# Loading x with four neighbouring tokens per partition, and putting the transposed tile back into token order as it leaves PSUM

## The chip, the cores and the metric

The kernel runs on one core of a Trainium2 chip. The metric is the device time of one execution in microseconds (us). A core has a matrix engine (PE; its weight loads are listed apart as PEld), a vector engine (DVE), a scalar engine (ACT), a general engine (POOL) and a sequencer that issues DMAs (SP). ACT and POOL can issue DMAs too. Data lies in HBM, is worked on in SBUF (128 partitions), and matrix products arrive in PSUM, which is used here as eight banks of 128 x 512 floats. Everything is float32.

## What is computed

x has 32 batches of 512 tokens with 256 channels, adj is a 512 x 512 matrix of zeros and ones per batch. With one layer norm in front, a graph layer is added to x:

```python
h = jnp.maximum(_layernorm(x, axis=-1), 0.0)
x = x + _L0_gnn_ref(h, adj, ...)
# inside the layer, with h as x:
xc = transpose(x, (0, 2, 1))
c = relu(bn1(conv1d(xc, conv1_w, 0)))            # 1 tap: a product per token
c = bn2(conv1d(c, conv2_w, 8))                   # 17 taps along the tokens
x_conv = transpose(relu(c + xc), (0, 2, 1))
s = x @ w_se.T + b_se                            # 3 numbers per token
A = exp(-|s_n - s_m|^2) * mask
x_nmp = A @ relu(x @ w_msg.T + b_msg)
# then a GRU cell: gates from x_in = [x_conv, x_nmp] and from x, out = (1 - z) * n + z * x
```

Two things of this matter for the change. The layer norm works on each token alone, so it doesn't matter in which partition a token lies. The 17-tap convolution runs along the tokens, so what comes after the transposition needs the tokens in their order.

## The kernel before

The batches are worked in two groups of 16 (g = 0 and 1, `GB` = 16). Each group has a first part (`first_part`, L1167) and a node part (`nodes`, L1322). After both groups a last part makes the gates and the output for pairs of batches. Tiles and names: P = 128, NC = 4 chunks of 128 tokens, DC = 2 halves of 128 channels, N = 512 tokens, D = 256 channels.

The first part does, for each batch:

- `load_x` (L213): one DMA of 512 KB brings x of the batch into a tile of 128 partitions x 4 chunks x 256 channels. Token c * 128 + p lies in partition p, chunk c. So a partition receives four runs of 1 KB. The loads of batches 1 to 5 and of 16 to 18 are issued by SP, the other 23 by POOL. Batch 0 is loaded in three pieces (L1298, L1299): chunk 0 and chunks 2 to 3 by SP, chunk 1 by ACT.
- `statistics` (L388): DVE takes mean and variance of each token (L392 four times, L394 four times, L397), and POOL raises the variance to the power -1/2 (`rstd`, L398).
- `normalise` (L400): xn = (x - mean) * rstd, four instructions on DVE (L411). In batches 0 (two chunks) and 17 (all four), ACT does it (L409).
- `transpose_h` (L414): PE transposes xn by 128 x 128 blocks, eight in all (L419, tile phT), four into each of two PSUM banks. So a bank holds 128 channels x 512 tokens, chunk after chunk. DVE moves each bank to SBUF and takes the maximum with 0 (L423, tile hT). For the second half of batch 0 ACT does it (L421). SP then stores hT to HBM (L424, tile hd), from where later parts read it.
- `conv1` (L430): 16 matrix products with hT as stationary side (L439, tile pc), moved out by DVE with an addition (L442, tile h), then made positive by ACT (L443).
- `windows_to_freq` (L447): 16 products that take the tokens into another domain for the 17-tap convolution (L454, tile px), moved out by ACT (L457, tile xf).

In group 0 the steps of `weights_to_freq` (L353) stand between these: they bring the convolution's weights into the same domain (PE L363, tile pw; moved out by ACT L373 and DVE L371, tile wst; stored by SP L377). In group 1 four leftover products of the first group (py, L503) and sums of weights on POOL and ACT (L1272) stand there.

The order is written out by hand (`manual_schedule`, L1316 and L1453); nothing is reordered. In a round b of group 1 the calls are: statistics of batch b + 2, transposition of batch b + 1, normalisation of b + 2, `conv1` of b, `windows_to_freq` of b - 1. On DVE that makes: stats (b + 2), hT (b + 1), xn (b + 2), h (b). On PE: phT (b + 1), pc (b), px (b - 1). Each engine takes its instructions in order, and waits for another engine by semaphores. `load_x` of batch b + 3 is issued at the head of round b. PSUM's eight banks are handed out in turn; such a round takes eight (two phT, two pc, four px).

Later parts load x of a batch again, in a layout of their own (tile xb); those loads are not those of `load_x`.

Of the kernel before, what the change touches and what calls it, by code (L numbers as in the profile page):

```python
# [12 lines left out]
AF = mybir.ActivationFunctionType  # L13
ALU = mybir.AluOpType

P = 128
# [146 lines left out]
def gnn_layer(  # L163
# [15 lines left out]
    nc = tc.nc  # L179
# [5 lines left out]
    NC = N // P  # L185
# [16 lines left out]
    def bank(name):  # L202
        return psum.tile([P, N], FP, tag="bank", name=name)

    X, ADJ, XN, HT, HQ, H1, MSG, A, NMP, ST, SL, SR = ({} for _ in range(12))
# [6 lines left out]

    def load_x(b, queue=nc.sync):  # L213
        X[b] = pools["ahead" if b == GB else "first"].tile([P, NC, D], FP, tag="x", name=f"x_{b}", bufs=1 if b == GB else 3)
        queue.dma_start(X[b], x[b].rearrange("(c p) d -> p c d", p=P))


    ident = consts.tile([P, P], FP, name="ident")
# [66 lines left out]
    def load_w1():  # L285

        t = W2P["w1"] = pools["gen"].tile([P, PI, D], FP, tag="w2p", name="w1_in", bufs=2)
        load_rows(t[:, :DC], w1T, nc.sync)
# [57 lines left out]
    def load_taps(gen, pc, queue=nc.gpsimd):  # L346
        t = W2P[pc] = gen.tile([P, PI, D], FP, tag="w2p", name=f"w2p_{pc}", bufs=2)
        src = w2T.rearrange("(q i) k o -> q k i o", q=4)[:, :, PI * pc : PI * (pc + 1)]
        for q in range(4):
            queue.dma_start(t[32 * q : 32 * q + 16], src[q, 0:16])  # L350
        queue.dma_start(t[16::32], src[:, 16])
# [62 lines left out]
    def transpose_h(b):  # L414
        HT[b] = work.tile([P, DC, N], FP, tag="hT", name=f"hT_{b}")
        for dc in range(DC):
            p = bank(f"phT_{b}_{dc}")
            for c in range(NC):
                nc.tensor.transpose(p[:, c * P : (c + 1) * P], XN[b][:, c, dc * P : (dc + 1) * P], ident)  # L419
            if b == 0 and dc > 0:  # L420
                nc.scalar.activation(HT[b][:, dc, :], p, AF.Relu)  # L421
            else:
                nc.vector.tensor_scalar(HT[b][:, dc, :], p, 0.0, None, op0=ALU.max)  # L423
        nc.sync.dma_start(HD[b], HT[b])  # L424
        del XN[b]

# [740 lines left out]
    def first_part(g, freq, between, left=()):  # L1167
# [3 lines left out]
        for b in range(b0, b0 + 3):  # L1171
            if b not in X and (g == 0 or b == b0):
                load_x(b)
# [22 lines left out]
        if g > 0:  # L1196
            place_h1(b0)
            load_x(b0 + 1)
            fill()
            load_x(b0 + 2)  # L1200
        transpose_h(b0)
        statistics(b0 + 1)
        fill()
# [4 lines left out]
        for b in range(b0, b1):  # L1208
            if b + 3 < b1:
                load_x(b + 3, nc.sync if b < 3 else nc.gpsimd)  # L1210
            if b == b0:
                conv1(b)
                one, two = between(0) if g == 0 else ([], [])
                for step in one:
                    step()
                fill()
                if g == 0:
                    transpose_h(b + 1)
                    statistics(b + 2)
                    normalise(b + 2)  # L1220
                else:
                    normalise(b + 2)
                    transpose_h(b + 1)
                fill()
                xf, last_two = freq(g), two
                continue
# [54 lines left out]
    @contextmanager  # L1281
    def phase(*names, bufs=1):
        with ExitStack() as stack:
            for name in names:
                pools[name] = stack.enter_context(tc.tile_pool(name=name, bufs=bufs, reuse_waits="tile"))
            yield

    with tc.tile_pool(name="freq", bufs=1) as fpool:
# [3 lines left out]
        with phase("first", "gen"):  # L1292
            gen = pools["gen"]
            per = N // D
            steps = [partial(weights_to_freq, gen, pc, i) for pc in range(QI // PI) for i in range(0, PI, per)]

            X[0] = pools["first"].tile([P, NC, D], FP, tag="x", name="x_0", bufs=3)
            for queue, c0, c1 in ((nc.sync, 0, 1), (nc.scalar, 1, 2), (nc.sync, 2, NC)):  # L1298
                queue.dma_start(X[0][:, c0:c1, :], x[0, c0 * P : c1 * P, :].rearrange("(c p) d -> p c d", p=P))  # L1299
            load_w1()  # L1300
            load_x(1)
            load_taps(gen, 0, nc.sync)
            nc.sync.dma_start(taps, nc.inline_tensor(taps_np, name="dft_taps").ap())
            nc.sync.dma_start(fwd, nc.inline_tensor(fwd_np, name="dft_fwd").ap())

            def between(b):
                if 1 <= b <= len(load_weights):
                    load_weights[b - 1]()

                n = (2, 0, *(3 if b in (12, 14) else 2 for b in range(2, GB)))[b]  # L1310
                mine = [[steps.pop(0)] for _ in range(n)]
                if b % 2 == 0 and b // 2 + 1 < QI // PI:
                    mine[b > 0].insert(0, partial(load_taps, gen, b // 2 + 1))
                return (mine[0], mine[1:]) if b == 0 else mine

            with tc.manual_schedule():  # L1316
                xf = first_part(0, freq_tile, between)
# [232 lines left out]
```

## Time and profile before

| | |
|---|---|
| time, median of three runs | 1731.43 us (1731.42 to 1732.1) |
| the profiled execution's own time | 1730.94 us |
| its span, first to last instruction | 1729.2 us |
| L423, hT from PSUM, DVE, 128 x 512 | 63 instructions, mean 685 ns |
| L421, hT from PSUM, ACT, 128 x 512 | 1 instruction, 597 ns |
| L411, xn, DVE, 128 x 256 | 122 instructions, mean 452 ns |
| L392, stats, DVE, 128 x 256 | 128 instructions, mean 410 ns |
| L442, h from PSUM, DVE, 128 x 512 | 64 instructions, mean 683 ns |
| x, issue of a load on POOL (L215) | 23, median 798 ns |
| x, issue of a load on SP (L215) | 8, median 431 ns |
| x, from issue to landing | median 6.4 us (3.7 to 9.5) |
| idle time of DVE that ended with a landing of x | 10.5 us, 10 times |

The page of the profile gives the busy time of each engine, the span in 40 slices, the DMA queues, the chain of work that ended last, and the costliest groups of instructions with their mean duration and with the idle time just before them. Further views of the same execution list instructions in order of time, the waits by what ended them, and the busy time of the engines in chosen stretches. A busy PE is not a PE at its peak, as matrix products overlap. An instruction's duration includes its start-up, and the next one of the same engine can begin before it ends: two of the 685 ns take 1.29 us together. The first part of group 0 takes about 0 to 150 us, that of group 1 about 424 to 535 us.

### The profile page before, as it was taken

What the parts mean: (1) busy time and instruction counts of PE and PEld (TensorE: products, weight loads), DVE (VectorE), ACT (ScalarE), POOL (GpSimd) and SP (SyncE); (2) the same over time, 40 slices, a digit from 0 to 9 for tenths busy, and PEclk for the clock granted to TensorE, in tenths of its full rate; (3) what the DMA queues carried; (4) which work ended last, traced back from release to release, by engine and by line L of the source; (5) the groups of instructions that cost most, each with busy time, mean ns of one, the idle gap of its engine ahead of it and who ended that gap; (6) DMA issues with size and microseconds to landing.
All of it is one profiled execution on the core that took longest, in us unless ns stands there. A gap on an engine that the chain in (4) does not pass through costs nothing.

```text
span 1729.2 us, 24317 instructions
## 1 busy us (share of the span) xinstructions
PE 1715.6 (99%) x7920; PEld 1321.8 (76%) x7920; DVE 1304.2 (75%) x2599; ACT 692.2 (40%) x1669; POOL 1087.2 (63%) x1074
## 2 busy tenths in 40 slices
PE   9999999999999999999999999999999999999998
PEld 6777888888998888887877778777877787778754
DVE  7876877777996677666587778777887778777867
ACT  4556655553446555554323232232313331323221
POOL 3331787687655677777767657665667556755551
PEclk9999999999999999999999999999999999999999
DMA  9989987885878888898433454335523553345423
GB/s 256 301 279 264 262 232 240 259 228 181 275 245 230 268 241 246 230 257 305 120 103 74 80 128 113 73 72 128 128 66 67 125 128 87 75 96 128 111 55 73
DMA packets 311681, 295.07 MB, mean 171 GB/s; under 512 B 147436, under 2 KB 241164, under 8 KB 311172
## 3 DMA queue, kind: packets, MB, share of 16 engines
q1 hardware_dynamic: 301588, 265.17, 55.9%
q0 software_dynamic: 6960, 26.65, 4.9%
q10 hardware_dynamic: 3008, 1.72, 0.3%
q8 instruction: 63, 1.03, 0.3%
q14 instruction: 62, 0.51, 0.1%
HBM read 194.31 MB, written 99.16 MB: 170 GB/s over the span
## 4 chain that ended last, share of the span: by engine, by line
PE 95%; DVE 3%; DMA 1%; SPq 1%; POOL 1%; ACT 0%; issue 0%; DVEq 0%; POOLq 0%; ACTq 0%
PE pg L915 29%; PE pn L932 16%; PE py L503 11%; PE pn L670 10%; PE pm L558 6%; PE pc L439 6%; PE pc L878 4%; PE px L454 3%; PE pd L608 2%; PE pw L363 1%; PE phT L419 1%; PE pg L932 1%; PE pz L932 1%; PE pc L881 1%; PE pn L653 1%; DVE xn L411 0%
## 5 line engine op out<-in xcount | busy, mean ns | idle before, releaser
L470 POOL TENSOR_TENSOR wsum<-wt 128x512 f32<-128x512 f32 x66 | 94.2, 1427 | 99.6 <-DMA wt<-wd 64.0
L503 PE MATMUL py<-wt,xf 128*128 128x256 f32 x640 | 154.2, 384 | 0.0
L915 PE MATMUL pg<-te,sw 128*128 128x256 f32 x600 | 154.0, 379 | 0.0
L906 ACT ACTIVATE rz<-rz,brz 128x256 f32<-128x256 f32 x180 | 86.4, 504 | 146.7 <-DVE rz L921 146.7
L503 PEld LDWEIGHTS py<-wt,xf 128*128 128x128 f32 x640 | 117.1, 190 | 34.9 <-issue 19.7
L915 PEld LDWEIGHTS pg<-te,sw 128*128 128x128 f32 x600 | 114.0, 190 | 15.5
L915 PE MATMUL pg<-hn,sw 128*128 128x256 f32 x480 | 123.2, 379 | 0.0
L915 PE MATMUL pg<-tn,sw 128*128 128x256 f32 x480 | 123.2, 379 | 0.0
L618 DVE TENSOR_TENSOR A<-A,at 128x512 f32<-128x512 f32 x124 | 116.6, 979 | 6.4 <-ACT A L614 2.8
L932 PE MATMUL pn<-tn,sw_n 128*128 128x512 f32 x256 | 120.3, 592 | 0.0
L1077 ACT ACTIVATE pn<-nt,vech 128x512 f32<-128x512 f32 x45 | 31.1, 692 | 219.2 <-DVE nt L1074 139.8
L439 PE MATMUL pc<-w,hT 128*128 128x256 f32 x512 | 117.5, 382 | 0.9 <-DVE hT L423 0.9
L558 PE MATMUL pm<-wmsg,hq 128*128 128x259 f32 x512 | 117.4, 381 | 0.0
L439 PEld LDWEIGHTS pc<-w,hT 128*128 128x128 f32 x512 | 94.7, 190 | 23.6 <-issue 6.4
L812 POOL TENSOR_TENSOR tn<-hn 128x512 f32<-128x512 f32 x64 | 87.1, 1382 | 35.5 <-PE pn L932 35.5
L558 PEld LDWEIGHTS pm<-wmsg,hq 128*128 128x128 f32 x512 | 96.5, 189 | 14.6
L915 PEld LDWEIGHTS pg<-hn,sw 128*128 128x128 f32 x480 | 91.1, 190 | 18.3 <-PE pn L932 3.3
L915 PEld LDWEIGHTS pg<-tn,sw 128*128 128x128 f32 x480 | 91.2, 190 | 12.4
L921 DVE TENSOR_TENSOR ct<-pg,ct 128x256 f32<-128x256 f32 x180 | 74.8, 415 | 32.5 <-PE pg L915 22.7
L932 PEld LDWEIGHTS pn<-tn,sw_n 128*128 128x128 f32 x256 | 48.6, 190 | 61.2 <-issue 50.9
L932 PE MATMUL pn<-hn,sw_n 128*128 128x512 f32 x192 | 90.5, 593 | 0.2 <-DVE pn L1073 0.2
L915 PE MATMUL pg<-tec,sw 128*128 128x256 f32 x300 | 89.2, 379 | 0.0
(235 smaller groups left out, 4331.4 us busy)
## 6 DMA issues: line engine op xcount, KB each, us to landing
wt<-wd SPq DMA_DIRECT2D x80, 512.0 KB, 6.2
adj<-in_adj_dram SPq DMA_DIRECT2D x128, 256.0 KB, 5.8
wd<-wst SPq DMA_DIRECT2D x64, 320.0 KB, 5.5
yd<-y SPq DMA_DIRECT2D x76, 256.0 KB, 5.1
hd<-hT SPq DMA_DIRECT2D x32, 512.0 KB, 4.9
nd<-nmp SPq DMA_DIRECT2D x32, 512.0 KB, 3.0
xb<-in_x_dram SPq DMA_DIRECT2D x128, 128.0 KB, 6.1
out_dram<-xb SPq DMA_DIRECT2D x122, 128.0 KB, 2.8
```

The source lines that it names most:

```text
L439: nc.tensor.matmul(p[:, j, :], HT[b][:, ic, c * P : (c + 1) * P], w1[:, ic, :], start=(ic == 0), stop=(ic == DC - 1))
L470: nc.gpsimd.tensor_tensor(t, WT[g, u][:, 0], WT[g, u][:, 1], op=ALU.add)
L503: nc.tensor.matmul(dst, v[:, ic, :], w[:, ic, :], start=(ic == 0), stop=(ic == DC - 1))
L558: nc.tensor.matmul(p[:, : D + NS], hq[:, ic, c * P : (c + 1) * P], wmsg[:, ic, :], start=(ic == 0), stop=(ic == DC - 1))
L618: nc.vector.tensor_mul(A[b][:, mc, :], EXP.pop((b, mc)), AT.pop((b, mc)))
L670: nc.tensor.matmul(bk, left[:, k, :], right[:, k, :], start=(first and k == 0), stop=(k == 1), skip_group_check=True)
L812: nc.gpsimd.tensor_tensor(dst[:, k], x[:, k], y[:, k], op=op)
L878: nc.tensor.matmul(bk[:, t0:t1], YT[p][:, j, c, oc * P : (oc + 1) * P], back[:, n : n + t1 - t0], start=(c == 0), stop=False, skip_group_c ...
L906: nc.scalar.activation(at(dst), at(src), AF.Sigmoid, bias=brz[:, o : o + 1], scale=sign)
L915: nc.tensor.matmul(bk, SW["hk"][:, k, s, :], c if k == 2 else hn[:, k], start=(onto is None and k == 0), stop=(k == K3 - 1), skip_group_ch ...
L921: nc.vector.tensor_tensor(at(dst), at(x), at(y), op=op)
L932: nc.tensor.matmul(bk[:, t], weight(q, k, o), terms[k][q][:, t], start=(first and i == 0), stop=(i == len(ks) - 1), skip_group_check=True)
```

## The change

In the SBUF tile of x, partition p now holds the four neighbouring tokens 4p to 4p + 3: token 4p + c lies in chunk c. In HBM these are 4 KB in one run. Layer norm and transposition are done as before on this tile, so a PSUM bank of phT now holds the tokens in the order 0, 4, 8, ..., 508, 1, 5, ... The instruction that moves it to SBUF reads PSUM straight through and writes column m of chunk c to token 4m + c: neighbouring elements of its stream are written four floats apart. hT is as it was before, and so is everything after it. The three pieces of batch 0's load keep their chunks, and take them from the same rearranged view.

```diff
     def load_x(b, queue=nc.sync):
...
-        queue.dma_start(X[b], x[b].rearrange("(c p) d -> p c d", p=P))
+        queue.dma_start(X[b], x[b].rearrange("(p c) d -> p c d", p=P))
...
                 nc.tensor.transpose(p[:, c * P : (c + 1) * P], XN[b][:, c, dc * P : (dc + 1) * P], ident)
+            dst, src = HT[b][:, dc, :].rearrange("p (m c) -> p c m", c=NC), p.rearrange("p (c m) -> p c m", c=NC)
             if b == 0 and dc > 0:
-                nc.scalar.activation(HT[b][:, dc, :], p, AF.Relu)
+                nc.scalar.activation(dst, src, AF.Relu)
             else:
-                nc.vector.tensor_scalar(HT[b][:, dc, :], p, 0.0, None, op0=ALU.max)
+                nc.vector.tensor_scalar(dst, src, 0.0, None, op0=ALU.max)
...
             for queue, c0, c1 in ((nc.sync, 0, 1), (nc.scalar, 1, 2), (nc.sync, 2, NC)):
-                queue.dma_start(X[0][:, c0:c1, :], x[0, c0 * P : c1 * P, :].rearrange("(c p) d -> p c d", p=P))
+                queue.dma_start(X[0][:, c0:c1, :], x[0].rearrange("(p c) d -> p c d", p=P)[:, c0:c1, :])
```

The order of the instructions on each engine, their number and what they wait for are the same in both programs.

## The prediction

> **What bounds the kernel now.** I read the page's first parts first. The profiled execution took 1730.94 us, of which 1729.2 us are the span; 1.7 us lie around it. The median of the three runs shown is 1731.43, 0.5 us (0.03%) above it. My sum is made against 1730.94.
>
> ```profile
> span 1729.2 us, 24317 instructions
> PE 1715.6 (99%) x7920; PEld 1321.8 (76%) x7920; DVE 1304.2 (75%) x2599; ACT 692.2 (40%) x1669; POOL 1087.2 (63%) x1074
> ```
>
> PE has 13.6 us of idle in all, so there is little to gain anywhere. What can be lost must be read per stage: the changed lines run only in the two first parts, 0 to 150 us (batches 0 to 15) and 424 to 530 us (16 to 31). So I asked for the busy time of each engine in stretches there (columns: stretch, its length, then PE, PEld, DVE, ACT, POOL busy, clock, DMA share, GB/s).
>
> ```profile
> 20.00:40.00 20.00, 19.41 (x118) 13.95 (x115) 19.84 (x58) 10.44 (x24) 7.37 (x10) 1.00 0.95 268
> 453.40:516.70 63.30, 63.30 (x389) 59.17 (x388) 60.69 (x171) 29.78 (x85) 41.30 (x73) 1.00 0.76 266
> ```
>
> DVE, 75% over the span, is 99% busy in the first and 96% in the second of these stretches (and 93% to 99% in the 20 us slices from 440 to 520). There it is a second bound beside PE. The chain of work that ended last, cut to the first 60 us, shows DVE as the bound before 34.5 us (start, length, what):
>
> ```profile
> 15.33 1.19 DVE hT L423 x2
> 16.52 1.31 DVE stats L392 x4
> ...
> 23.88 1.29 DVE hT L423 x2
> ...
> 29.41 1.29 DVE hT L423 x2
> ...
> 33.93 0.48 ACT wst L373
> 34.41 0.04 issue
> 34.46 1.14 PE phT L419 x8
> ```
>
> Up to 34.46 the chain steps from DVE to DVE, and the evictions hT (L423) of batches 1, 2 and 3 are links of it. From there to 150 us it is mostly PE, whose pieces of one batch (phT 0.87, pc 3.65, px 2.37, two pw 1.03) sum to 8.95 us, against 7.2 us of DVE work (busy 54.57 us from 72 to 140, which is 7.6 batches). In the second first part the chain is all PE, one batch in 6.50 us:
>
> ```profile
> 459.65 0.87 PE phT L419 x8
> 460.53 3.46 PE pc L439 x16
> 463.98 2.17 PE px L454 x16
> 466.16 0.87 PE phT L419 x8
> ```
>
> From the start of batch 21's statistics (453.35) to that of batch 31's (516.68), by the timeline, DVE does ten batches with 60.69 us busy: 6.07 us each against PE's 6.50. That margin of 0.43 us per batch is the number on which all turns. The timeline shows how tight the coupling is: batch 21's xn (L411) ends at 459.16 and PE's transposes, which need it, start at 459.36.
>
> ```profile
> 457.15 2.01 DVE L411 TENSOR_SCALAR xn<-x,mv,rstd 128x256 f32<-128x256 f32 x4 [0.62 <-POOL rstd L398]
> 459.36 0.93 PEld L419 LDWEIGHTS phT<-ident,xn 128*128 128x128 f32 x8
> ```
>
> **The change, part by part.** No instruction is added, removed or moved on any engine; only the access patterns differ.
>
> *Loads of x.* Thirty-one loads of 512 KB become one 4 KB run per partition in place of four of 1 KB. Most wait nowhere: DVE idles for x 10.5 us in all (10 times), and PE waits for none of it except in the first 9 us. The loads from POOL, 23 of these 31, already travel as large packets:
>
> ```profile
> q0 software_dynamic: 6960, 26.65, 4.9%
> ```
>
> 26.65 MB in 6960 packets is 3.8 KB each; 23 loads at 1 KB would be 11776 packets alone. In the trace's packets 1 KB takes 46 ns and 4 KB 159 ns (medians), so a load from SP goes from 32 x 46 = 1.47 to 8 x 159 = 1.27 us per DMA engine: 0.2 us, beside PE. An issue on POOL (0.80 us) may come near that of other large POOL loads (hn 0.72 to 0.74): 0.06 us ahead of the rstd queued behind it. The first tile's three pieces keep 1 KB (two) and get 2 KB (one; 84 ns against 2 x 46); its statistics start at 2.98 and 4.41 us and PE waits for them, so here -0.2 to +0.3 us. The rest of the gain is bounded by PE's lost time that is near x: four batches from 34.46 to 71.77 take 37.3 us against 4 x 8.95 = 35.8, so 1.5 us at the most. I take 0 for the loads, with ends -1.7 and +0.3.
>
> *Evictions of the transposed tile.* 63 on DVE (L423, mean 685 ns) and one on ACT (L421, 597 ns) now write each 4-byte element 16 bytes from the last. Reads from PSUM stay contiguous. The trace has no such write of any length. Its rows:
> - DVE fills: contiguous 128 elements 165 ns, 16 elements each 32 bytes apart 72 ns.
>
> ```profile
> L326 DVE MEMSET fl<- 128x128 f32 x1 | 0.2, 165 | 0.8 <-PEq L1538 0.8
> L328 DVE MEMSET fl<- 128x16 f32 x1 | 0.1, 72 | 0.0
> ```
>
> A DVE element costs 1.05 ns by the 512- and 256-wide PSUM evictions (L442 683, L561 414 ns: 269 over 256). Sixteen contiguous ones would then take 165 - 112 x 1.05 = 47 ns; the strided fill took 25 more, 1.5 ns an element. For 512 elements that is +0.79 us per eviction: the upper end. Small instructions also carry some 40 ns that lines through large ones miss (L397, 4 elements, 169 ns at least, against 395 - 252 x 1.05 = 130 from L411's shortest), so the fill does not exclude +0.
> - ACT's xf copy (L457) reads PSUM 320 bytes apart and writes runs of four: 438 ns for 320 elements, on the line through its 256- and 512-wide copies (L677 374 and L655 587 give 427). [...]
>
> I take c = +0.54 us per eviction (512 x 1.05, a second step for each element), the round value between these ends that is nearest to the only DVE row with a strided write; ends 0 and 0.79.
>
> [...]
>
> **The sum for c = 0.54.** *First part:* batch 0's DVE eviction ends 0.21 us before the next statistics, which waited for x: 0.54 - 0.21 = 0.33. Then the six evictions of batches 1 to 3 stand in the chain: 6 x 0.54 = 3.24. Batch 0's ACT eviction runs beside DVE: its users (pc of batch 0, then h at 14.05) come behind xn of batch 1, so 0. From batch 4 on, two evictions make the 7.2 us of DVE per batch 8.3, against 8.95: covered by PE. With 0.65 us less of that cover they would begin to be paid. Sum 3.6.
>
> *Second part:* the eviction of batch 20 lies ahead of xn of batch 21. Its 1.08 is met by the 0.62 us in which xn waited for POOL's rstd, and by 0.2 to 0.33 before PE's transposes: 0.13 is left. Then each of ten batches needs 6.07 + 1.08 = 7.15 us of DVE, 71.5 in all, where PE took 65.0 from phT of batch 21 to phT of 31: 6.5. Batches 17 to 19 have gaps (DVE waited 1.62, 1.13 and 0.64 us for x between 426 and 454) that take their part, and hT of batch 31 ends at 526.44, with pc at 531.0: covered. Sum 6.6.
>
> Behind a slower eviction on SP stand the store hd (L424) and, behind that, stores of wst and early x loads; the store waits for DVE, and x of batch 3 and 4 is used by the same delayed DVE, so they add nothing. PSUM: the bank of a phT is asked for by PE a batch later, for transposes that need an xn which stands behind this eviction on DVE anyway: 0.
>
> Total 3.6 + 6.6 = +10.2 us: 1730.94 + 10.2 = **1741.1**.
>
> **Rivals.**
> 1. *The strided write runs at full rate (c under about 0.3), so not slower.* At c = 0 DVE is as before; loads give -1.7 to +0.3: 1729.2 to 1731.2. Decides: the total passes 3.5 us (0.2%) near c = 0.3 (first part 7 x 0.3 - 0.21 = 1.9, second 10 x (6.07 + 0.6) - 65.0 = 1.7). For it: ACT's xf row, small-instruction overhead in the fill.
> 2. *The fill's full price, c = 0.79.* First part 0.58 + 4.74 = 5.3; second 10 x (6.07 + 1.58) - 65.0 + (1.58 - 0.95) = 12.1: 1748.3.
> 3. *The loads do more than I allow (faster).* Every wait for x that reaches PE would have to vanish, and some that the profile doesn't show, as 1.7 is under 3.5. Against it: PE 99%, packets on q0 already large.
> That the change doesn't do what it says is part of rival 1: for POOL's loads the larger runs may change nothing, being packets of that size now.
>
> **How the numbers follow.** About 0.2%, 3.5 us, is what a measurement of this kernel can tell from no change. Forecast (c 0.3 to 0.65): 0.48, its own range 1734.5 to 1745. Rival 1: 0.40. Rival 2 (over 0.65): 0.08. Rival 3: 0.04. So slower 0.56, same 0.40, faster 0.04. Cases of both signs hold most of the chance, so the range goes from 1729.2 (rival 1's low end) to 1748.3.
>
> **What would show it.** L423's mean: near 685 ns says rival 1, about 1.22 us the forecast, about 1.47 rival 2. If the forecast holds, the stretch 453 to 517 shows DVE near 100%, batches 21 to 31 at about 7.15 us in place of 6.50, PE with waits for xn, and phT of batch 4 starts near 38 us, not 34.46. The forecast is wrong if L423 grows and these don't move: then DVE had more room than its busy time tells. Loads: issues of L215 on POOL under 0.80 us, DVE waits for x under 10.5 us.

## The result, and the profile after

The changed kernel takes 1736.96 us (median of 9 runs, 1734.72 to 1741.0) against 1731.42 (9 runs, 1729.5 to 1733.47): ratio 1.0031, 95% interval 1.0022 to 1.004. It is slower by 5.5 us; the forecast was 1741.1 in a range of 1729.2 to 1748.3. Its profiled execution took 1735.49 us, 4.55 more than that of before, with a span 4.5 us longer. So the trace below shows somewhat less than the median loss. Of the nine runs, the four with a mean granted clock of 0.999 (the clock that PE was granted, as a share of its full speed) took 1734.72 to 1736.96 us, the five with 0.996 to 0.998 took 1735.51 to 1741.0, and the trace is of one of the four.

The page of the changed kernel, its first two lines:

```profile
span 1733.7 us, 24317 instructions
PE 1717.1 (99%) x7920; PEld 1321.2 (76%) x7920; DVE 1314.9 (76%) x2599; ACT 691.8 (40%) x1669; POOL 1081.6 (62%) x1074
```

The same instructions run; DVE is busy 10.7 us longer. The busy time by stretch (same columns as before; the second is again ten batches, from the statistics of batch 21 to those of 31):

```profile
20.00:40.00 20.00, 19.46 (x113) 13.10 (x112) 18.85 (x52) 10.11 (x23) 7.97 (x11) 1.00 0.92 244
...
458.00:523.50 65.50, 65.50 (x403) 61.18 (x402) 64.94 (x171) 30.20 (x86) 39.43 (x73) 1.00 0.72 255
```

In the ten batches DVE is busy for 64.94 us, where it had 60.69: 6.49 per batch, with PE at 6.5. It has caught up with PE, and has not passed it. The evictions themselves, before and after, now line L424 (one line further down; later lines too), by tile:

```profile
L423 DVE TENSOR_SCALAR hT<-phT x63: 674/681/694, 8.8 to 525.8; 128x512 f32<-128x512 f32 x63
L424 DVE TENSOR_SCALAR hT<-phT x63: 1056/1083/1205, 9.1 to 530.9; 128x512 f32<-128x512 f32 x63
```

Smallest, median and largest are in ns: 1083 where it was 681, so 0.40 us more, or 0.78 ns an element. The chain that ended last, in its first 40 us:

```profile
15.01 1.20 DVE h L443 x2
16.21 1.90 DVE hT L424 x2
18.11 1.21 DVE stats L392 x4
...
25.37 2.01 DVE hT L424 x2
...
31.48 1.31 DVE hT L424 x2
...
37.05 1.14 PE phT L419 x8
```

The links are those of before. The first pair of evictions takes 1.90 us of the chain (1.19 before), the second 2.01 (1.29). The third is named with 1.31 only, but from its start to the next xn it is 1.84 us (1.28). PE's transposes of batch 4 start at 37.05 us (34.46). Of the span's 4.5 us, 2.6 are lost by then.

The table gives the points of the traces from which I read where time is lost: the start in us of the statistics of batch 1 (DVE, L392), and of phT (PE, L419) of some batches, and the span. The experiments are in the next section.

| kernel | stats 1 | phT 4 | phT 16 | phT 19 | phT 21 | phT 31 | span |
|---|---|---|---|---|---|---|---|
| before | 9.71 | 34.46 | 424.29 | 446.49 | 459.49 | 524.52 | 1729.2 |
| changed | 10.60 | 37.05 | 427.31 | 450.38 | 463.41 | 528.66 | 1733.7 |
| e1, loads alone | 10.61 | 35.35 | 424.93 | 447.49 | 460.49 | 525.52 | 1730.3 |
| e2, evictions alone | 9.70 | 36.24 | 426.43 | 449.47 | 462.49 | 527.82 | 1733.5 |
| e3, stride on the PSUM read | 11.24 | 36.28 | 426.64 | 449.07 | 462.08 | 527.10 | 1731.2 |
| e4, stride on PE's write | 10.42 | 35.15 | 424.98 | 447.17 | 460.18 | 525.20 | 1730.8 |
| e5, table of patterns | 9.57 | 34.98 | 424.19 | 446.43 | 459.43 | 524.46 | 1728.7 |
| e6, two tokens | 10.77 | 35.49 | 424.60 | 447.25 | 460.25 | 525.45 | 1730.7 |
| e7, first tiles as before | 9.59 | 34.32 | 424.70 | 447.03 | 460.04 | 525.06 | 1729.6 |
| e8, one eviction more | 11.13 | 37.68 | 427.64 | 452.46 | 467.43 | 542.34 | 1748.2 |
| e9, before, half on ACT | 10.46 | 37.23 | 425.75 | 447.93 | 460.94 | 525.96 | 1730.8 |
| e10, e7, half on ACT | 10.12 | 37.20 | 426.01 | 448.20 | 461.20 | 526.23 | 1730.9 |
| e11, changed, half on ACT | 10.96 | 38.51 | 428.38 | 451.19 | 464.19 | 529.22 | 1734.6 |
| e12, changed again | 10.19 | 38.34 | 428.12 | 450.99 | 464.42 | 530.58 | 1734.8 |

Changed against before: 2.6 us by batch 4, 0.4 more by batch 16, 0.9 between batches 16 and 19, 0.3 from 19 to 31, 0.4 after. A trace is one execution, and small differences in this table are not told from chance: up to batch 16 e8 runs the same program as the changed kernel, and its phT of batch 4 comes 0.6 us later. The granted clock matters too. In 10 to 20 us it was 0.83 in e12, 0.89 in e3, 0.93 in e9 and 0.95 in e10, and 1.00 in the other rows; e11 fell to 0.91 in 20 to 40 us. At the lower clock the products of batch 1 (pc) took 5.41 us in e3, where they took 3.89 in e1, and those of batch 0 5.34 in e12, where they took 3.73 in the changed kernel. So the phT of batch 4 in these rows is later than the program alone would make it.

For the 0.9 the chains of both kernels show the place. Before:

```profile
437.55 2.59 PE py L503 x12
440.15 0.87 PE phT L419 x8
441.02 3.46 PE pc L439 x16
```

Changed:

```profile
440.57 1.26 PE py L504 x6
441.82 1.29 DVE xn L411 x4
443.11 1.92 DVE hT L424 x2
445.04 0.04 issue
445.08 3.29 PE pc L440 x14
```

Here PE's products of batch 17 need the hT that DVE has only just made: before, hT ended at 440.86 and pc began at once, without delay for PE; now PE waits for it. e2 loses 0.85 us there; e1, e3 and e6 lose 0.2 to 0.5, e4 nothing.

### The profile page after: what moved, and what is told of

It reads as the page before. It is cut to its first block, busy times and chain, and to the rows that moved or that the text cites. A ratio compares the mean times of both kernels' runs of the same rounds, so it can differ in the third digit from the quotient of the medians.

```text
span 1733.7 us, 24317 instructions
## 1 busy us (share of the span) xinstructions
PE 1717.1 (99%) x7920; PEld 1321.2 (76%) x7920; DVE 1314.9 (76%) x2599; ACT 691.8 (40%) x1669; POOL 1081.6 (62%) x1074
## 3 DMA queue, kind: packets, MB, share of 16 engines
q0 software_dynamic: 6960, 26.65, 4.9%
## 4 chain that ended last, share of the span: by engine, by line
PE 93%; DVE 3%; DMA 1%; POOL 1%; issue 1%; ACT 0%; SPq 0%; ACTq 0%; DVEq 0%; POOLq 0%
PE pg L916 29%; PE pn L933 16%; PE py L504 11%; PE pn L671 10%; PE pm L559 6%; PE pc L440 5%; PE pc L879 4%; PE px L455 3%; PE pd L609 2%; PE pw L363 1%; PE phT L419 1%; PE pg L933 1%; PE pz L933 1%; PE pc L882 1%; PE pn L654 1%; DMA x<-in_x_dram 1%
## 5 line engine op out<-in xcount | busy, mean ns | idle before, releaser
L398 POOL TENSOR_TENSOR rstd<-rstd,minus_half 128x4 f32<-128x4 f32 x32 | 33.4, 1043 | 94.0 <-DVE rstd L397 89.1
```

## The experiments

Theory W: the time is lost because the strided write makes DVE's eviction longer, first where DVE is in the chain. Its main rival, L, puts it on the loads. A theory M on the second group was added: the change has just used up DVE's margin there.

**e1, the loads alone, and e2, the evictions alone.** In both, hT holds the tokens in a wrong order. e1:

```diff
-            dst, src = HT[b][:, dc, :].rearrange("p (m c) -> p c m", c=NC), p.rearrange("p (c m) -> p c m", c=NC)
+            dst, src = HT[b][:, dc, :], p
```

e2 keeps the strided write and has both loads of before (`x[b].rearrange("(c p) d -> p c d", p=P)`, and the three pieces as they were).

> Four neighbouring tokens per partition are loaded, but the tile leaves PSUM straight, so hT holds the tokens in permuted order. Theory W (the strided writes cost the time): L423's successor stays at about 685 ns, the time is that of before plus at most 1 us (0 to 0.06%), phT of batch 4 starts within 1 us of 34.46 us. Rival L (the loads cost the time: the first pieces and x of batch 1 land later): +3 us or more over before, phT of batch 4 at 36 us or later, with statistics of batch 1 at about 10.6 us as in the changed kernel (9.71 before).

> x is loaded as before, and the tile leaves PSUM with the strided write, so hT holds the tokens in permuted order. Theory W: eviction about 1085 ns, +3.5 to +5 us over before, phT of batch 4 at 36.5 to 37 us, ten batches 21 to 31 still at 6.50 to 6.55 us each. Rival L: +2.5 us or less, phT of batch 4 before 36 us.

Measured beside 1731.39 us for before: e1 1731.78 us, ratio 1.0003 (0.9994 to 1.0012); e2 1735.44 us, 1.0025 (1.0016 to 1.0034). The evictions alone bring 4.05 of the 5.5 us, the loads alone 0.4, which is not told from none; the 1.1 us missing from the sum of both lies within the intervals. W holds, L falls as the main cause. In the traces, e2's phT of batch 4 is 1.8 us late, and it has the 0.9 between 16 and 19; in the second group it shows nearly the same busy time of DVE as the whole change:

```profile
457.00:522.50 65.50, 65.50 (x403) 61.15 (x402) 64.75 (x170) 30.15 (x87) 41.11 (x72) 1.00 0.72 256
```

e1's trace has 0.9 us lost by batch 4, from the start: its statistics begin at 3.35 and 5.01 us (2.98 and 4.41 before). In e4 and e6, at the same clock, it is 0.7 and 1.0.

**e3 and e4, the same permutation elsewhere.** e3 writes SBUF straight and reads PSUM with neighbouring elements 128 floats apart; e4 lets PE write PSUM four floats apart, and moves the tile straight.

```diff
 e3
-            dst, src = HT[b][:, dc, :].rearrange("p (m c) -> p c m", c=NC), p.rearrange("p (c m) -> p c m", c=NC)
+            dst, src = HT[b][:, dc, :].rearrange("p (m c) -> p m c", c=NC), p.rearrange("p (c m) -> p m c", c=NC)
 e4
-                nc.tensor.transpose(p[:, c * P : (c + 1) * P], XN[b][:, c, dc * P : (dc + 1) * P], ident)
+                nc.tensor.transpose(p.rearrange("p (m c) -> p c m", c=NC)[:, c, :], XN[b][:, c, dc * P : (dc + 1) * P], ident)
-            dst, src = HT[b][:, dc, :].rearrange("p (m c) -> p c m", c=NC), p.rearrange("p (c m) -> p c m", c=NC)
+            dst, src = HT[b][:, dc, :], p
```

> All of the change, but DVE and ACT write hT straight through and read PSUM with neighbouring elements 128 floats apart. Theory W (it is the write into SBUF that is slow, as ACT's xf copy reads PSUM 320 bytes apart at full rate): eviction about 685 ns, time as with the loads alone, 0 to +1 us over before. Rival R (any stride in the pattern slows the eviction): about 1085 ns or more and +5 us as in the changed kernel.

> All of the change, but the transposes themselves write PSUM with neighbouring elements four floats apart, and the tile leaves PSUM straight. If PE's strided writes into PSUM are free: phT at 0.87 us for eight as before, eviction about 685 ns, 0 to +1 us over before. If they take twice as long as now: eight transposes 1.7 us, so +0.85 us for each of 28 batches in which PE is the bound, about +24 us.

Measured: e3 1731.70 us, 1.0004 (0.9995 to 1.0013); e4 1731.99 us, 1.0002 (0.9993 to 1.0011). Both give the change's layout without its loss. The eviction in e3, and PE's transposes in the kernel before and in e4:

```profile
L424 DVE TENSOR_SCALAR hT<-phT x63: 675/682/692, 9.1 to 528.3; 128x512 f32<-128x512 f32 x63
```

```profile
L419 PE MATMUL phT<-ident,xn x256: 272/273/331, 7.6 to 525.3; 128*128 128x128 f32 x128
L419 PE MATMUL phT<-ident,xn x256: 272/273/329, 8.0 to 526.0; 128*128 128x128 f32 x128
```

682 ns is the eviction of before (681), and a transpose takes 273 ns in both. So the rival that any stride slows the eviction falls: it is the write into SBUF.

**e5, a table of patterns.** The loads are the change's. The pattern goes by batch modulo 8, the first half of the channels leaves on DVE and the second on ACT; hT holds permuted tokens. The edit is shortened here: its comments stand for eight branches, with the lines that DVE and ACT run.

```diff
-            dst, src = HT[b][:, dc, :].rearrange("p (m c) -> p c m", c=NC), p.rearrange("p (c m) -> p c m", c=NC)
-            if b == 0 and dc > 0:
+            to = HT[b][:, dc, :]
+            k = b % 8   # L427/425 k=0: to, p (straight)
+            # written n apart: L433/431 n=2, L439/437 n=4, L445/443 n=8, L451/449 n=16, L457/455 n=64
+            #   to.rearrange("p (m c) -> p c m", c=n), p.rearrange("p (c m) -> p c m", c=n)
+            # L463/461: to.rearrange("p (m c) -> p m c", c=4), p.rearrange("p (c m) -> p m c", c=4)
+            # L469/467: to.rearrange("p (m c t) -> p c m t", c=2, t=2), p.rearrange("p (c m t) -> p c m t", c=2, t=2)
+            if dc > 0:
```

> Loads as in the change; the eviction's pattern is chosen by batch modulo 8, first half of the channels on DVE, second half on ACT, so hT holds permuted tokens: straight; elements written 2, 4, 8, 16 or 64 floats apart; straight write with PSUM read 128 floats apart; pairs of floats written 4 floats apart. Theory line (what costs is that every element opens a new 16 byte piece): straight 681 on DVE and about 600 on ACT, 2 apart the same or little more, 4, 8, 16 and 64 apart all about 1083 on DVE and 1075 on ACT, pairs no more than half of that addition (about 680 to 880), the PSUM read 681. Rival slope (the cost grows with the distance): 2 apart about 0.2 us more, 8, 16 and 64 apart clearly over 1083.

A single run took 1730.45 us. The instructions of the tile hT, smallest, median and largest in ns, on DVE:

```profile
L427 DVE TENSOR_SCALAR hT<-phT x4: 676/692/692, 9.0 to 479.6; 128x512 f32<-128x512 f32 x4
L433 DVE TENSOR_SCALAR hT<-phT x4: 677/686/693, 15.1 to 486.1; 128x512 f32<-128x512 f32 x4
L439 DVE TENSOR_SCALAR hT<-phT x4: 1071/1084/1110, 24.1 to 492.6; 128x512 f32<-128x512 f32 x4
L445 DVE TENSOR_SCALAR hT<-phT x4: 1081/1084/1090, 30.0 to 499.1; 128x512 f32<-128x512 f32 x4
L451 DVE TENSOR_SCALAR hT<-phT x4: 1022/1037/1048, 36.1 to 505.6; 128x512 f32<-128x512 f32 x4
L463 DVE TENSOR_SCALAR hT<-phT x4: 691/692/692, 45.3 to 512.3; 128x512 f32<-128x512 f32 x4
L469 DVE TENSOR_SCALAR hT<-phT x4: 692/693/693, 54.2 to 518.7; 128x512 f32<-128x512 f32 x4
L457 DVE TENSOR_SCALAR hT<-phT x4: 1028/1049/1055, 64.6 to 525.2; 128x512 f32<-128x512 f32 x4
```

and on ACT, straight, 2 and 4 floats apart, with PSUM read 128 floats apart, in pairs, and 64 floats apart:

```profile
L425 ACT ACTIVATE hT<-phT x4: 597/598/632, 9.4 to 480.1; 128x512 f32<-128x512 f32 x4
...
L431 ACT ACTIVATE hT<-phT x4: 626/641/659, 17.6 to 487.4; 128x512 f32<-128x512 f32 x4
...
L437 ACT ACTIVATE hT<-phT x4: 1084/1109/1142, 24.8 to 493.7; 128x512 f32<-128x512 f32 x4
...
L461 ACT ACTIVATE hT<-phT x4: 597/597/623, 46.0 to 512.6; 128x512 f32<-128x512 f32 x4
L467 ACT ACTIVATE hT<-phT x4: 624/650/673, 54.6 to 520.0; 128x512 f32<-128x512 f32 x4
L455 ACT ACTIVATE hT<-phT x4: 1042/1064/1087, 63.6 to 526.2; 128x512 f32<-128x512 f32 x4
```

Two floats apart, and pairs whose starts are four floats apart, cost DVE nothing (686 and 693 against 692), and ACT about 0.05 us (641 and 650 against 598). Single elements 4, 8, 16 or 64 floats apart take 1037 to 1084 ns on DVE, without growing with the distance. That is a step at one element per 16 bytes, as the theory had it; a slope with distance is refuted. The pairs, expected at no more than half of the addition, cost next to nothing.

**e6, two tokens per partition,** so 2 KB runs and elements two floats apart.

```diff
-        queue.dma_start(X[b], x[b].rearrange("(p c) d -> p c d", p=P))
+        queue.dma_start(X[b].rearrange("p (h t) d -> p h t d", t=2), x[b].rearrange("(h p t) d -> p h t d", p=P, t=2))
...
+            dst, src = HT[b][:, dc, :].rearrange("p (h m t) -> p h t m", h=2, t=2), p.rearrange("p (h t m) -> p h t m", h=2, t=2)
...
```

> Two neighbouring tokens per partition in place of four: runs of 2 KB in HBM, elements written two floats apart. Theory line: eviction 681 to 780 ns, time within 1 us of the loads alone (0 to +1.5 us over before). Rival slope: eviction about 0.2 us more and +2 to +3 us over before.

Measured: 1732.36 us beside 1731.89, ratio 1.0002 (0.9994 to 1.0011), with the eviction at 682 ns: as expected.

**e7, the first two tiles as before.** e3, but batches 0 and 1 are loaded and moved as before.

```diff
+        if b == 1:
+            queue.dma_start(X[b], x[b].rearrange("(c p) d -> p c d", p=P))
...
+            if b < 2:
+                dst, src = HT[b][:, dc, :], p
```

> As the read-side version, but batches 0 and 1 are loaded as before and leave PSUM straight; batches 2 to 31 have the four tokens per partition. Theory F (what the loads cost comes in the first 11 us, where the first pieces and x of batch 1 land later): statistics of batch 0 at 2.95 and 4.4, of batch 1 at 9.7, phT of batch 4 at 34.4 to 34.7 us, time that of before within 0.5 us. Rival: all loads cost a little, phT of batch 4 within 0.3 us of the read-side version's 36.28, +0.3 us or more over before.

Measured: 1730.88 us beside 1731.89, ratio 0.9996 (0.9987 to 1.0005); phT of batch 4 at 34.32 us. The trace agrees with F: with the first two tiles as before, nothing is lost by batch 4, where e1, e4 and e6, at the same granted clock, have 35.15 to 35.49 (e3's 36.28 came at a lower one). The time lies 1.0 us under that of before, where F allowed 0.5; this, and the difference to e3, are within the intervals, so the time shows neither.

**e8, one eviction more per batch in group 1.**

```diff
                 nc.vector.tensor_scalar(dst, src, 0.0, None, op0=ALU.max)
+            if b >= GB and dc == 0:
+                nc.vector.tensor_scalar(dst, src, 0.0, None, op0=ALU.max)
```

> The changed kernel with one more strided eviction per batch in group 1 (the first half's, written a second time with the same values): 16 instructions more, 0.92 us of DVE each. Theory M (in group 1 the change has just used up DVE's margin, 64.9 us busy in the 65.3 us of ten batches): nearly all of it is paid from batch 19 on, +8 to +12 us over the changed kernel (1745 to 1749), phT of batch 21 to phT of 31 about 73 to 74.5 us in place of 65.25. Rival S (there is slack that the busy time does not tell): under +5 us, under 69 us.

Measured: 1750.25 us (four runs), ratio 1.0108 (1.0093 to 1.0124) to before, 13.3 us over the changed kernel, slightly more than expected; phT of batch 21 to that of 31 takes 74.9 us. The busy times there, and some of the chain:

```profile
467.00:542.00 75.00, 73.65 (x403) 61.87 (x401) 74.31 (x181) 30.38 (x86) 36.79 (x69) 1.00 0.58 206
```

```profile
465.75 1.10 DVE hT L424
466.85 0.91 DVE xn L411 x2
467.76 0.04 issue
467.80 1.41 PE phT L419 x7
469.22 3.55 PE pc L442 x16
```

Now DVE is the bound: hT, then xn, then PE's transposes that wait for xn. This is the chain that I had forecast for the change itself. In the changed kernel's trace it does not form. In e12, the same program, it forms once, behind an x that landed late (DVE waited 1.7 us for x in the ten batches there, 0.4 in the changed kernel). M holds, and S falls.

**e9 to e11, half of the evictions on ACT,** in the kernel before (e9), in e7 (e10) and in the changed kernel (e11); and **e12, the changed kernel again** beside them.

```diff
-            if b == 0 and dc > 0:
+            if dc > 0:
```

> The kernel before, but the second half of the channels leaves PSUM on ACT in all batches, not only in batch 0. If DVE's chain of the first 34 us is what bounds that stretch, three evictions of 0.61 us leave it: phT of batch 4 at 32.6 to 33.9 us, -0.5 to -2 us over before; nothing in group 1, where PE is the bound. Rival: ACT, which has the weights' moves in its queue, hands hT over later and PE waits for it: 0 or slower.

> Four tokens per partition from batch 2 on (batches 0 and 1 as before), permuted on the PSUM read, and the second half of the channels leaves PSUM on ACT. If e7 and e9 add up: -1 to -2.5 us over before, the fastest here. Rival: the same as before within 0.5 us.

> The changed kernel with its strided writes, but the second half of the channels leaves PSUM on ACT in all batches. Theory M (what is paid is DVE's time, not the slow write as such): 31 slow writes move to an engine with room, DVE has 0.92 us less per batch, so group 1 costs nothing and the first 34 us about 1 us: 0 to +2 us over before. Rival P (PE waits for the slow write itself): +4 us or more, as with all of them on DVE.

> The changed kernel once more, beside these: +4 to +6 us over before (1.0022 to 1.004 in its first runs).

Measured beside 1731.62 us: e9 1732.53, ratio 1.0011 (1.0002 to 1.0019); e10 1732.69, 1.0011 (0.9998 to 1.0024); e11 1736.33, 1.0023 (1.0013 to 1.0034); e12 1736.65, 1.0033 (1.002 to 1.0045). e12 repeats the result. The hopes for e9 and e10 failed. In the second group e11 is as theory M has it: from phT of batch 21 to that of 31 it takes 65.03 us, exactly the time of before, with slow writes on both engines. Of the 5.4 us that its span is longer, 4.1 are lost by phT of batch 4 (38.51 us), and 0.6 between batches 16 and 19. e11's chain at the start:

```profile
15.38 0.61 DVE h L443
15.99 0.02 issue
16.01 1.23 ACT h L444 x2
17.24 1.92 ACT wst L373 x4
19.16 0.97 ACT hT L422
20.14 0.04 issue
20.18 4.98 PE pc L440 x14
```

On ACT the eviction stands behind h and four moves of wst, so PE gets hT of batch 1 at 20.1 us; pc of batch 1 had begun at 15.98 in the kernel before. e9 and e10, with straight writes, lose in the same place (phT of batch 4 at 37.23 and 37.20). But this wait is only a part of the loss. e5 also has half of its evictions on ACT, and its granted clock stayed at 1.00. The last 14 products of batch 1, in e5 and in e9:

```profile
18.34 3.29 PE L485 MATMUL pc<-w,hT 128*128 128x256 f32 x14 [1.80 <-ACT hT L431]
```

```profile
19.21 4.68 PE L439 MATMUL pc<-w,hT 128*128 128x256 f32 x14 [1.78 <-ACT hT L421]
```

PE waited 1.8 us for ACT in both, yet e5's phT of batch 4 came at 34.98, only 0.5 after before. What differs is the time of the products: 3.29 us in e5, 4.68 in e9 and 4.98 in e11, with the granted clock in 20 to 40 us at 1.00, 0.95 and 0.91. So 1.4 of the 2.8 us that e9 lost by batch 4, and 1.7 of e11's 4.1, came with the clock; why it fell is open. The statistics of batch 1, too, began 0.7 and 1.2 us later than before, where in e5 they did not. Nor does e11's total decide between M and P: two of its seven runs took 1732.39 and 1732.99 us, within what M allows, the other five 1736.08 to 1738.12, as P has it. None of these versions beats the kernel before beyond its interval; e7 has the lowest median, 1730.88.

## Why the prediction was right, and where it was off

The direction was right, and so was the mechanism in the first part: a longer write on DVE, paid where DVE is in the chain. In the second part the mechanism that was forecast, DVE setting the pace of every batch, did not appear. The size was half, 5.5 us of 10.2; the range held the result, but it was wide enough to hold no change as well. By its steps:

- *The price c.* Forecast 0.54 us per eviction, by taking a second step for each element: an estimate, and no run shows that step. Measured 0.40 in duration (1083 ns for 681), and less in what DVE is kept: from the first to the second eviction of a pair 0.608 us before and 0.923 now, so 0.32. The bounds 0 and 0.79, estimates too, held. This is the term that was mis-sized, and it is in both sums.
- *First part, forecast 3.6.* With c = 0.32 its own sum is 7 x 0.32 - 0.21 = 2.0; e2 shows 1.8 by phT of batch 4. The chain was right. That phT of batch 4 came at 37.05, near the 38 named as a sign, is partly luck: about 0.9 of the 2.6 us lost by then are the loads', which the sum had at nothing.
- *The loads, forecast 0, ends -1.7 and +0.3.* The end upwards was too near in the traces: by phT of batch 4, 0.9 us in e1 (0.7 in e4, 1.0 in e6). In time the four kernels with the new loads and fast evictions (e1, e3, e4, e6) stand at +0.3 to +0.6 us, none of them told from 0. What the load was to gain did not come: POOL's issue of a load fell from 0.80 to 0.60 us, as forecast in sign, but no time was won by it, and its queue moved 6960 packets as before. DVE idled 9.1 us for x in the changed kernel (10.5 before), but 12.7 in e1, so the loads did not shorten this wait.
- *Second part, forecast 6.6.* By the traces 1.1 from batch 16 to 31. Two steps failed. The sentence that batches 17 to 19 are covered by gaps was wrong: PE waits for hT of batch 17, and 0.9 us are lost there (0.85 in e2). And the ten batches from 21 to 31, forecast at 71.5 us, took 65.25. The signs named for it, 7.15 us per batch and waits of PE for xn, did not come: it was 6.53, without such a wait. With c = 0.32 the sum would be 10 x (6.07 + 0.64) - 65.0 = 2.1, and DVE's other work became shorter as well. Before and after, in the ten batches:

```profile
L411 DVE TENSOR_SCALAR xn<-x,mv,rstd 128x256 f32<-128x256 f32 x40 | 18.7, 528 | 0.6 <-POOL rstd L398 0.6
...
L423 DVE TENSOR_SCALAR hT<-phT 128x512 f32<-128x512 f32 x20 | 12.9, 685 | 0.4
```

```profile
L424 DVE TENSOR_SCALAR hT<-phT 128x512 f32<-128x512 f32 x20 | 20.2, 1087 | 0.0
L411 DVE TENSOR_SCALAR xn<-x,mv,rstd 128x256 f32<-128x256 f32 x40 | 17.4, 495 | 0.0
```

  xn takes 1.3 us less, all of it in the first of a batch's four: 518 ns in the mean before, 384 now. Before, six of these ten began 0.04 to 0.05 us after a sum of weights on POOL (L1272) did, and took 546 to 554 ns; two began 0.22 us after it and took 404. In the changed kernel the eight beside such a sum began 0.19 to 0.24 us after it and took 375 to 414. So the slower eviction moved xn against POOL's work, and that paid for a part of it, which the sum did not foresee; that POOL is the cause was not tested. The 0.43 us of margin per batch was all but enough: DVE was busy 6.49 us of the 6.53 that a batch took (6.50 before). e8 shows that the next 0.92 us is paid almost in full, and e12, the same program, lost 1.1 us in these ten batches (66.16 us): at the edge it varies from run to run. This may be a part of the 1.0 us between the trace's 4.5 and the median's 5.5, and the granted clock of the runs another.
- *Covered costs.* From batch 4 to 16 the forecast cover held but for 0.4 us. The eviction on ACT (597 to 1072 ns) was not separated.
- *Rivals.* Rival 1 (full rate) is refuted by 1083 ns, rival 2's price by the same; rival 3 by e1.

Open: why the new loads land later at the start. In all nine traces with the new first loads (the changed kernel, e1, e3 to e6, e8, e11, e12) the first statistics start at 3.11 to 3.41 us, in the five with the old ones (before, e2, e7, e9, e10) at 2.88 to 2.98; the first piece now gathers 1 KB rows that lie 4 KB apart (2 KB in e6), where it was 128 KB in one run. That this is the cause was not tested. For the statistics of batch 1 the two overlap (9.6 to 11.2 against 9.6 to 10.5).

## What to carry to other kernels

A permutation that an eviction must make belonged here on the PSUM read (e3, 682 ns an eviction, as straight) or on the matrix engine's PSUM write (e4, 273 ns a transpose, as straight), not on the SBUF write, where single floats 16 bytes apart took 1083 ns in place of 681. A margin per round (here 0.43 us) tells whether a small cost is free; an engine at 96% in a stretch is one such cost away from being the bound, and e8 shows the price right behind it (13.3 us for 16 evictions more). Moving work to an engine with idle time need not help: in e9 PE waited 1.8 us for an eviction on ACT that stood behind ACT's other work. And before a loss in one trace is put down to such a wait, the granted clock of the stretch is to be compared: in e9 half of the loss by batch 4 (1.4 of 2.8 us) came with it.

## What the runs showed of the hardware

Writing single floats into SBUF 16 or more bytes apart cost about the same on the two engines that did it: on DVE an eviction of 128 x 512 took 1.04 to 1.08 us where it took 0.69 straight (e5), and with 16 bytes it was 0.923 us from one eviction to the next, 1.80 ns an element (0.608 and 1.19 straight); ACT took 1.04 to 1.14 us where it took 0.60. The time did not grow with the distance from 16 to 256 bytes (1084 and 1049 ns on DVE, 1109 and 1064 on ACT), and 8 bytes apart was free on DVE (686 ns beside 692). Reads from PSUM 512 bytes apart cost neither engine anything (692 and 597 ns, beside 692 and 598 straight), and PE's writes into PSUM 16 bytes apart took the 273 ns of straight ones. The same 14 products of PE took 3.29 us at a granted clock of 1.00, and 4.68 and 4.98 where it was 0.95 and 0.91 in the mean of 20 to 40 us.
